# Last attention of a decoder stack: how the queries' maxima reach every partition, and how far the exponentials run behind the scores

## The chip, the cores and the metric

The kernel runs on one core of a Trainium2 chip. The metric is the device time of one execution in microseconds (us). Three runs of the kernel before took 2780.61, 2783.06 and 2793.99 us; the median is 2783.06 us.

## The reference, cut to what matters

A stack of twelve layers (four rounds of self attention, cross attention and a feed-forward part) works on `x` of shape 4 x 256 x 128, with a context of 4 x 1601 x 96. The change touches only the second last layer, a cross attention with 16 heads of 64, which the last layer follows, a linear map whose weights and inputs are whole numbers of eight bits:

```python
def _L3_xattn_ref(x, context, Wq, Wk, Wv, Wo, bo):
    HEADS, DIM_HEAD = 16, 64
    b, n, _ = x.shape                      # 4, 256, 128
    h, d = (HEADS, DIM_HEAD)
    scale = d ** (-0.5)
    q = (x @ Wq).reshape(b, n, h, d).transpose(0, 2, 1, 3)
    k = (context @ Wk).reshape(b, -1, h, d).transpose(0, 2, 1, 3)   # 1601 keys
    v = (context @ Wv).reshape(b, -1, h, d).transpose(0, 2, 1, 3)
    sim = jnp.einsum('bhid,bhjd->bhij', q, k) * scale
    attn = jax.nn.softmax(sim, axis=-1)
    out = jnp.einsum('bhij,bhjd->bhid', attn, v)
    out = out.transpose(0, 2, 1, 3).reshape(b, n, h * d)
    return out @ Wo + bo

x = _layernorm(x + _L3_xattn_ref(x, ctx_768, ...), axis=-1)
x = _layernorm(x + _L3_ffn_ref(x, weight_q, weight_scale, bias), axis=-1)
```

The softmax is over all 1601 keys, and the maximum over the keys is subtracted from each query's scores before the exponential. All of this is in 32-bit floats.

## The kernel before, in words

The kernel is one program of eight stages, one after the other on the same core; the last stage, `l3_xattn`, begins at about 1908 us of the span. A helper, `mm` (L389), issues almost every product of TensorE, so nearly all products carry its line and are told apart by their tiles.

**Units and steps.** The work is cut into 32 units, one batch and one pair of heads each, the two heads standing in the two halves of the 128 partitions. The 1601 keys are 13 chunks of up to 128 keys. A unit takes four steps of up to four chunks; `parts(g)` gives a step's tiles of two chunks each, so steps 0, 1 and 2 of a unit have two tiles and step 3 has one, with the last 65 keys. Scores lie transposed: the keys on the partitions, the 256 queries (two blocks of 128, `NB` = 2) of both heads along the free dimension. One tile `St` holds 2 heads x 2 chunks x 256 queries, 1024 numbers per partition.

**What each part does.** `queries` makes Q of a unit (TensorE; VectorE copies it out of PSUM, L1890). `projections` makes K of the coming step and V of the step whose exponentials are due (ScalarE copies both, L1921). `scores` multiplies Q and K; ScalarE copies each tile from PSUM to `St` in SBUF (L1933). `running` keeps a maximum over the tiles of a unit, element by element, in a place of an old weight tile (VectorE, L1940 and L1943; the trace calls this place w), and at the unit's end joins the two chunks to `mx` (L1947). `maxima` turns that over with products with the identity, so that the queries come onto the partitions, and VectorE reduces over the 128 key partitions (L1959): `mq` has 128 queries on the partitions and 4 columns, one per head and block of queries. `spread` must bring these 512 maxima onto every partition: 8 products of a column of `mq`, broadcast to 64, with the identity put them into a PSUM tile, and ScalarE copies it to `Mb` (L1971). `shifted` subtracts `Mb` from each score tile (VectorE, L1977), `weights` takes the exponential in place (ScalarE, L1984), and `sums` multiplies the exponentials with V and with ones, adding up over a unit in one PSUM tile. At a unit's end the denominators are copied (`rows`, L2016), spread by a product, inverted and multiplied in (VectorE, L2025 and L2028), and after each batch's eighth unit the output projection, the norms and the last layer follow a few instructions at a time (`advance(later)`).

**The order.** TensorE, VectorE and ScalarE run this stage in the order in which it is written (`manual_schedule`), each from its own queue, waiting on semaphores. The loop at the end of `l3_xattn` lays down step g: scores are made for step g, while subtraction and exponential work on step g - LAG and `sums` on the step before that; LAG is 5. There are 12 tiles `St` to hold what lies between. Two PSUM tiles called `one` serve queries, maxima, spread, the sums and the output; three wider ones, `big`, serve projections and scores.

SP issues the DMAs. In this stage it issues only the two small loads at the start and the write of each batch's output (L2112). The weights `Wq`, `Wk` and `Wv` of this stage (pack p4, 3072 columns) lie in the weight slot `w0`, whose widest tenant earlier in the program has 4224 columns.

Of the kernel before, what the change touches and what calls it, by code (L numbers as in the profile page):

```python
# [21 lines left out]
B, T, D = 4, 256, 128  # L22
P = 128
NB = T // P
# [4 lines left out]
NH = 16  # L29
# [15 lines left out]
SW = 32  # L45
# [3 lines left out]
SLOT = {  # L49
    "p0": 0, "down": 0, "p4": 0, "p1": 1, "p3_0": 1, "p5": 1, "p2": 2, "p3_1": 2,  # L50
    "up": 3, "p3_2": 3, "gp": 4, "p3_3": 4,
}

SINGLES = ("l0_xattn", "block1", "l2_xattn", "l2_ffn", "l3_attn")

# [5 lines left out]
class Pack:  # L61


    def __init__(self, width):
        self.a = np.zeros((P, width), np.float32)
        self.at = {}
        self.n = 0
# [236 lines left out]
class Net:  # L304
    def __init__(self, ctx: ExitStack, tc: tile.TileContext, dram, at):
        self.tc, self.nc, self.dram, self.at = tc, tc.nc, dram, at

        def pool(name, bufs, **kw):
            return ctx.enter_context(tc.tile_pool(name=name, bufs=bufs, **kw))

        self.const = pool("const", 1)
        self.wpool = pool("wpool", 1)
        self.act = pool("act", 2)
        self.stage = None
        self.packs = {}
        self.carried = []
        self.n = 0
# [35 lines left out]
    def load(self, name, keep=False, parts=(0,)):  # L353
        src = self.dram[name]
        if keep:
            t = self.tile(name, [P, src.shape[1]], pool=self.const)
        else:
            t = self.tile(f"w{SLOT[name]}", [P, src.shape[1]], pool=self.wpool)
        for lo, hi in zip(parts, parts[1:] + (src.shape[1],)):
            self.nc.sync.dma_start(t[:, lo:hi], src[:, lo:hi])  # L360
        self.packs[name] = t
# [1493 lines left out]
    def l3_xattn(self):  # L1855
# [2 lines left out]

        nc = self.nc
        HD, LAG = 64, 5
        halves = [slice(0, HD), slice(HD, P)]
        wq, wk, wv = self.w("p4", "Wq"), self.w("p4", "Wk", CD), self.w("p4", "Wv", CD)
        units = [(b, hp) for b in range(B) for hp in range(NH // 2)]
        steps = 4 * len(units)
        qs, ks, vs, sts, mx, top, accs, outs = {}, {}, {}, {}, {}, {}, {}, {}
# [5 lines left out]
        kept = self.tile(f"w{SLOT['p3_1']}", [P, 11, T], pool=self.wpool)  # L1873
        one = [kept[:, i].rearrange("p (n d) -> p n d", n=NB) for i in range(8, 11)]
        places = {"h": kept[:, 4:8], "x1": one[0], "x3": one[1], "xn": one[2]}
        self.late = places.get

        def parts(g):

            d = g % 4  # L1880
            for k in range(2 * d, min(2 * d + 2, NCH // 2 + 1)):
                yield k, min(2, NCH - 2 * k), min(P, S2 - 2 * k * P)
# [40 lines left out]
        def scores(g):  # L1923
            u = g // 4
            for k, nc_, kp in parts(g):
                ps = self.big().rearrange("p (h c t) -> p h c t", h=2, c=2)
                for c in range(nc_):
                    o = (2 * k + c - g % 4 * 4) * P
                    for h, r in enumerate(halves):
                        self.mm(ps[:kp, h, c, :], ks[g][r, o : o + kp], qs[u][r, :])  # L1930
                st = self.tile("St", [P, 2, 2, T], bufs=12)
                sts[u, k] = st
                nc.scalar.copy(st[:kp, :, :nc_, :], ps[:kp, :, :nc_, :])  # L1933

        def running(g):
            u = g // 4
            for k, nc_, kp in parts(g):
                if k == 1:
                    mx[u] = kept[:, :4].rearrange("p (h c) t -> p h c t", h=2)
                    nc.vector.tensor_max(mx[u], sts[u, 0], sts[u, 1])  # L1940
                elif k:
                    to = mx[u][:kp, :, :nc_, :]
                    nc.vector.tensor_max(to, to, sts[u, k][:kp, :, :nc_, :])  # L1943
            if g % 4 == 3:
                m = mx.pop(u)
                mx[u] = self.tile("mx", [P, 2, T], bufs=2)
                nc.vector.tensor_max(mx[u], m[:, :, 0, :], m[:, :, 1, :])  # L1947

        def maxima(u):

            ps, m = self.misc(), mx.pop(u)
            for h in range(2):
                for n in range(NB):
                    o = (h * NB + n) * P
                    for d in halves:
                        cols = slice(n * P + d.start, n * P + d.stop)
                        self.mm(ps[d, o : o + P], m[:, h, cols], self.ident)
            mx[u] = self.tile("mq", [P, 2 * NB], bufs=2)
            nc.vector.reduce_max(out=mx[u], in_=ps.rearrange("p (j k) -> p j k", k=P), axis=AX.X)  # L1959

        def spread(u):

            ps, m = self.misc(), mx.pop(u)
            for j in range(2 * NB):
                for d in halves:
                    self.mm(
                        ps[d, j * P : (j + 1) * P],
                        m[:, j : j + 1].broadcast_to([P, HD]), self.ident,
                    )
            top[u] = self.tile("Mb", [P, 2, T], bufs=2)  # L1970
            nc.scalar.copy(top[u].rearrange("p h t -> p (h t)"), ps)  # L1971

        def shifted(g):
            u = g // 4
            for k, nc_, kp in parts(g):
                e = sts[u, k][:kp, :, :nc_, :]
                nc.vector.tensor_sub(  # L1977
                    e, e, top[u][:kp].unsqueeze(2).broadcast_to([kp, 2, nc_, T])
                )

        def weights(g):
            for k, nc_, kp in parts(g):
                e = sts[g // 4, k][:kp, :, :nc_, :]
                nc.scalar.activation(e, e, AF.Exp, scale=HD**-0.5)  # L1984

        def sums(g):
            u = g // 4
            if g % 4 == 0:
                accs[u] = self.misc()
            acc = accs[u]  # L1990
            es = [(k, nc_, sts.pop((u, k))[:kp]) for k, nc_, kp in parts(g)]
            for k, nc_, e in es:
                for c in range(nc_):
                    i = 2 * k + c
                    for h, d in enumerate(halves):
                        if i < NCH - 1:
                            self.mm(
                                acc[d, :T], vs[g][:, i - g % 4 * 4, d], e[:, h, c, :],
                                start=i == 0, stop=False,
                            )  # L2000
            for k, nc_, e in es:
                kp = e.shape[0]
                for c in range(nc_):
                    for h in range(2):
                        d = slice(HD * h + SW * c, HD * h + SW * c + SW)
                        self.mm(
                            acc[d, T:], self.w("c", "ones", kp)[:, :SW], e[:, h, c, :],
                            start=False, stop=False,
                        )
                if kp < P:  # L2010
                    for h, d in enumerate(halves):
                        self.mm(acc[d, :T], vs[g][:kp, 0, d], e[:, h, 0, :], start=False)
            vs.pop(g)
            if g % 4 == 3:
                rows = self.tile("rows", [P, T], bufs=1)
                nc.scalar.copy(rows, acc[:, T:])  # L2016
                later.append(ended(u, rows))
# [32 lines left out]
        with self.tc.manual_schedule(engines=engines):  # L2050
            for g in range(-1, steps + LAG + 2):
                gb = g - LAG
                if g % 4 < 2 and 0 <= g - 1 < steps:
                    running(g - 1)
                if g % 4 == 1 and 4 < g <= steps + 1:
                    spread(g // 4 - 1)
                if 0 <= gb < steps:
                    shifted(gb)
                if 0 <= g + 1 < steps and (g + 1) % 4 == 0:
                    queries((g + 1) // 4)  # L2060
                if g + 1 < steps or gb < steps:
                    projections(g + 1, gb)
                if 0 <= gb < steps:
                    weights(gb)
                self.advance(later)
                if 0 <= gb - 1 < steps:
                    sums(gb - 1)
                if g % 4 == 0 and 4 <= g <= steps:
                    maxima(g // 4 - 1)
                if g % 4 > 1 and 0 <= g - 1 < steps:  # L2070
                    running(g - 1)
                if 0 <= g < steps:
                    scores(g)
            while later:
                self.advance(later)
# [59 lines left out]
```

## Time and profile before

| | |
|---|---|
| median of three runs | 2783.06 us |
| the profiled execution | 2780.11 us |
| its span, first to last instruction | 2778.3 us |
| TensorE busy | 2620.5 us (94%) |
| VectorE busy | 1747.2 us (63%) |
| ScalarE busy | 1526.2 us (55%) |
| mean granted TensorE clock | 0.977 |

The profile gives one execution, with engines named PE (TensorE products), PEld (TensorE weight loads), DVE (VectorE), ACT (ScalarE), POOL (GpSimd) and SP (the engine that issues the DMAs). A group line names the source line, the engine, the operation, output and inputs, the shapes, the count, then after a bar the busy time in us and the mean of one in ns, then the idle time of the engine just before these instructions and what ended it. A timeline line has the start and the length in us, the engine, and in brackets the idle time before. In the row of 40 slices each digit is the busy share of one slice in tenths; a slice is 69.5 us.

### The profile page before, as it was taken

To read this page: it belongs to the slowest core of one execution; us is meant where nothing else is said; L and a number is where in the kernel's file an instruction comes from. 1 tells how busy PE (TensorE), PEld (TensorE's weight loads), DVE (VectorE), ACT (ScalarE), POOL (GpSimd) and SP (SyncE) were. 2 spreads that over 40 slices of the span, in tenths; PEclk is the share of its full clock that TensorE was granted. 3 is DMA by queue.
4 is the path that set the end of the run, shared out by engine and by line. 5 is a ranking of instruction groups with operands and counts; after the bars stand their busy time and mean duration, and the time that the engine had idled before them with its cause. 6 is when DMAs were issued, how large, how long until landed. Compare 5 with 4: busy or idle time off the path is not lost.

```text
span 2778.3 us, 63280 instructions
## 1 busy us (share of the span) xinstructions
PE 2620.5 (94%) x26619; PEld 1707.8 (61%) x26619; DVE 1747.2 (63%) x3802; ACT 1526.2 (55%) x2931; POOL 180.8 (7%) x199
## 2 busy tenths in 40 slices
PE   6999999988879999999997999999999999999997
PEld 4555565555555555555796777776566666666665
DVE  5656666365457666655344666666767777777775
ACT  2555555535533555555553555556666566566563
POOL 2000100120020000000001011101000000000000
PEclk8999999989989999999998999999999999999999
DMA  3000000000020000000002000000000000000000
GB/s 111 2 1 1 2 1 1 3 21 15 26 88 13 6 1 1 1 2 1 1 1 91 15 25 13 12 13 3 2 1 2 3 2 2 3 2 1 3 2 3
DMA packets 12955, 34.57 MB, mean 12 GB/s; under 512 B 3832, under 2 KB 7036, under 8 KB 11264
## 3 DMA queue, kind: packets, MB, share of 16 engines
q1 hardware_dynamic: 12672, 30.53, 3.9%
q8 instruction: 210, 3.44, 0.5%
q14 instruction: 73, 0.60, 0.1%
HBM read 23.67 MB, written 0.52 MB: 9 GB/s over the span
## 4 chain that ended last, share of the span: by engine, by line
PE 88%; DVE 6%; ACT 3%; issue 2%; POOL 1%; DMA 1%; DVEq 0%; POOLq 0%; ACTq 0%
PE one L389 63%; PE big L389 13%; PE acc L389 8%; DVE M L899 1%; PE one L825 1%; PE one L534 1%; PE one L462 1%; DVE St L1977 1%; DVE mpad L687 1%; PE one L1314 1%; ACT E L721 0%; DMA QK<-qk 0%; DVE w L1943 0%; DVE rec L2025 0%; POOL rn L1247 0%
## 5 line engine op out<-in xcount | busy, mean ns | idle before, releaser
L899 DVE TENSOR_REDUCE M<-one 128x1 f32<-128x458 f32 (+3 forms) x1024 | 528.7, 568 | 291.7 <-PE one L389 290.2
L922 ACT ACTIVATE E<-one 128x512 f32<-128x512 f32 (+1 forms) x896 | 457.7, 563 | 422.5 <-PE one L389 422.4
L389 PE MATMUL one<-Q,K 32*128 32x256 f32 (+1 forms) x3328 | 531.9, 402 | 1.5 <-DVE M L899 1.5
L389 PE MATMUL one<-K,Q 32*128 32x458 f32 (+3 forms) x2048 | 458.8, 543 | 1.6 <-DVE M L899 1.6
L389 PEld LDWEIGHTS one<-Q,K 32*128 32x128 f32 (+1 forms) x3328 | 310.7, 180 | 62.4 <-DVE M L899 35.5
L1933 ACT COPY St<-big 128x1024 f32<-128x1024 f32 (+1 forms) x224 | 204.3, 959 | 160.1 <-PE big L389 160.1
L389 PEld LDWEIGHTS one<-K,Q 32*128 32x128 f32 x2048 | 171.1, 186 | 143.3 <-issue 79.7
L1977 DVE TENSOR_TENSOR St<-St,Mb 128x1024 f32<-128x1024 f32 (+1 forms) x224 | 245.3, 1142 | 1.8 <-ACT Mb L1971 1.8
L389 PE MATMUL acc<-E,V 128*32 128x256 f32 (+1 forms) x3328 | 233.2, 387 | 7.1 <-ACT E L922 7.1
L1984 ACT ACTIVATE St<-St 128x1024 f32<-128x1024 f32 (+1 forms) x224 | 215.1, 1014 | 26.0 <-DVE St L1977 25.9
L721 ACT ACTIVATE E<-one 128x384 f32<-128x384 f32 (+1 forms) x352 | 154.3, 525 | 111.9 <-PE one L389 111.7
L389 PE MATMUL big<-Q,K 64*128 64x256 f32 (+1 forms) x1664 | 214.4, 393 | 0.0
L482 POOL TENSOR_TENSOR ln_r<-ln_ve,half 128x2 f32<-128x2 f32 x92 | 70.9, 770 | 2080.0 <-DVE ln_ve L480 2025.7
L389 PE MATMUL one<-St,V 128*64 128x256 f32 (+1 forms) x1664 | 204.1, 382 | 0.4
L1943 DVE TENSOR_TENSOR w<-w,St 128x1024 f32<-128x1024 f32 (+1 forms) x160 | 178.6, 1116 | 35.2 <-ACT St L1933 27.4
L682 DVE TENSOR_REDUCE Ms<-one 128x3 f32<-128x384 f32 x256 | 130.3, 551 | 97.3 <-PE one L389 96.1
L389 PE MATMUL one<-xT,w 128*128 128x256 f32 (+1 forms) x664 | 169.5, 396 | 18.8 <-DVE Q L1117 8.3
L389 PEld LDWEIGHTS big<-Q,K 64*128 64x128 f32 (+1 forms) x1664 | 147.7, 183 | 57.5 <-issue 40.6
L389 PEld LDWEIGHTS acc<-E,V 128*32 128x32 f32 (+1 forms) x3328 | 87.3, 109 | 125.0 <-issue 70.0
L389 PEld LDWEIGHTS one<-St,V 128*64 128x64 f32 (+1 forms) x1664 | 113.5, 137 | 62.7 <-issue 14.6
L389 PE MATMUL one<-QK 32*128 32x256 f32 (+1 forms) x1408 | 110.7, 385 | 24.3 <-DMA QK<-qk 13.7
L389 PEld LDWEIGHTS big<-w,ctx 96*64 96x64 f32 x1664 | 97.1, 137 | 54.0 <-issue 53.9
(308 smaller groups left out, 3733.5 us busy)
## 6 DMA issues: line engine op xcount, KB each, us to landing
w<-in_p SPq DMA_DIRECT2D x4, 1096.0 KB
QK<-qk SPq DMA_DIRECT2D x256, 16.0 KB
rows<-in_ctx_rows SPq DMA_DIRECT2D x4, 630.5 KB
ctx<-in_ctx SPq DMA_DIRECT2D x4, 600.4 KB
w<-in_down SPq DMA_DIRECT2D x1, 2112.0 KB
w<-in_up SPq DMA_DIRECT2D x1, 1632.0 KB
w<-in_gp SPq DMA_DIRECT2D x1, 1632.0 KB
w<-in_p SPq DMA_DIRECT2D x1, 1536.0 KB
```

Of the source, the lines that this page charges most:

```text
L389: self.nc.tensor.matmul(out, lhsT, rhs, start=start, stop=stop)
L462: self.nc.tensor.transpose(ps[:, n * P : (n + 1) * P], x[:, n, :], self.ident)
L482: nc.gpsimd.tensor_tensor(rstd, ve, self.half[:, :NB], ALU.pow)
L534: self.nc.tensor.transpose(ps[:rows, n * P : (n + 1) * P], m4[:, n, :rows], self.ident)
L682: nc.vector.reduce_max(out=m[:, j, :], in_=ps[:, : 3 * P].rearrange("p (s c) -> p s c", c=P), axis=AX.X,)
L721: nc.scalar.activation(es[t, j], ps[:, :w], AF.Exp, scale=scale)
L899: nc.vector.reduce_max(out=ms[i][:, n, j, part : part + 1], in_=ps[:, at : at + hi - lo], axis=AX.X)
L922: nc.scalar.activation(e[:kp, :w], ps[:kp, :w], AF.Exp, scale=scale)
L1933: nc.scalar.copy(st[:kp, :, :nc_, :], ps[:kp, :, :nc_, :])
L1943: nc.vector.tensor_max(to, to, sts[u, k][:kp, :, :nc_, :])
L1977: nc.vector.tensor_sub(e, e, top[u][:kp].unsqueeze(2).broadcast_to([kp, 2, nc_, T]))
L1984: nc.scalar.activation(e, e, AF.Exp, scale=HD**-0.5)
```

## The change

`spread` no longer uses TensorE and ScalarE. The small tile `mq` (128 queries x 4) is written by one DMA to a row in DRAM, in the order query, then head and block, and a second DMA reads that row of 512 numbers back onto all 128 partitions. It lands in one of two places `home`, which are 1024 columns added to the pack p4's tile in the weight slot. `spread` is called right after `maxima`, one step earlier than before. Since the row's fastest index is now head and block, `shifted` reads it with a view that makes the query the inner index, with a step of four elements; for that view the score tiles change their order from head, chunk, query to chunk, head, query, which changes the indices in `scores`, `running`, `weights` and `sums`. LAG becomes 6 and the tiles `St` 14.

```diff
+SPARE = {"p4": 1024}
...
+        self.dram_pool = pool("dram", 2, space=bass.MemoryType.DRAM)
...
-            t = self.tile(f"w{SLOT[name]}", [P, src.shape[1]], pool=self.wpool)
+            wide = src.shape[1] + SPARE.get(name, 0)
+            t = self.tile(f"w{SLOT[name]}", [P, wide], pool=self.wpool)
...
-        HD, LAG = 64, 5
+        HD, LAG = 64, 6
...
+        home = self.packs["p4"][:, 3 * NH * HD :].rearrange("p (i c) -> p i c", i=2)
...
-                st = self.tile("St", [P, 2, 2, T], bufs=12)
+                st = self.tile("St", [P, 2, 2, T], bufs=14)
                 sts[u, k] = st
-                nc.scalar.copy(st[:kp, :, :nc_, :], ps[:kp, :, :nc_, :])
+                nc.scalar.copy(
+                    st[:kp, :nc_, :, :].rearrange("p c h t -> p h c t"), ps[:kp, :, :nc_, :]
+                )
...
-            ps, m = self.misc(), mx.pop(u)
-            for j in range(2 * NB):
-                for d in halves:
-                    self.mm(
-                        ps[d, j * P : (j + 1) * P],
-                        m[:, j : j + 1].broadcast_to([P, HD]), self.ident,
-                    )
-            top[u] = self.tile("Mb", [P, 2, T], bufs=2)
-            nc.scalar.copy(top[u].rearrange("p h t -> p (h t)"), ps)
+            row = self.tile("mrow", [P, 2 * NB], bufs=2, pool=self.dram_pool)
+            nc.sync.dma_start(row, mx.pop(u))
+            top[u] = home[:, u % 2]
+            nc.sync.dma_start(
+                top[u], row.rearrange("t j -> (t j)").unsqueeze(0).broadcast_to([P, 2 * T])
+            )
 
         def shifted(g):
             u = g // 4
+            m = top[u].rearrange("p (t j) -> p j t", j=2 * NB).unsqueeze(1)
             for k, nc_, kp in parts(g):
-                e = sts[u, k][:kp, :, :nc_, :]
-                nc.vector.tensor_sub(
-                    e, e, top[u][:kp].unsqueeze(2).broadcast_to([kp, 2, nc_, T])
-                )
+                e = sts[u, k][:kp, :nc_].rearrange("p c h (n t) -> p c (h n) t", n=NB)
+                nc.vector.tensor_sub(e, e, m[:kp].broadcast_to([kp, nc_, 2 * NB, P]))
...
-                if g % 4 == 1 and 4 < g <= steps + 1:
-                    spread(g // 4 - 1)
...
                 if g % 4 == 0 and 4 <= g <= steps:
                     maxima(g // 4 - 1)
+                    spread(g // 4 - 1)
```

## The prediction

> **What bounds the kernel now.** I read first the page's head and its 40 slices, to see which engine is full where the change works. The last stage fills the slices from about 28 on.
>
> ```profile
> PE 2620.5 (94%) x26619; PEld 1707.8 (61%) x26619; DVE 1747.2 (63%) x3802; ACT 1526.2 (55%) x2931; POOL 180.8 (7%) x199
> ...
> PE   6999999988879999999997999999999999999997
> ...
> DVE  5656666365457666655344666666767777777775
> ACT  2555555535533555555553555556666566566563
> ```
>
> TensorE is full, VectorE at seven tenths. Then the busy times by window over two successive units (one batch and one pair of heads each), with columns stretch, length, PE, PEld, DVE, ACT, POOL, clock, DMA share, GB/s:
>
> ```profile
> 2191.30:2215.88 24.58, 24.58 (x268) 15.44 (x266) 19.82 (x23) 16.86 (x24) 0.00 (x0) 1.00 0.02 7
> 2215.88:2240.46 24.58, 24.58 (x269) 15.43 (x266) 17.93 (x19) 16.85 (x24) 0.00 (x0) 1.00 0.01 2
> ```
>
> A unit takes 24.58 us and TensorE is busy in all of it, at full granted clock: whatever leaves TensorE shortens a unit, until another engine's 17 to 20 us grow past it. Third, the groups of lines between 1990 and 2700 us, for the pieces that the change touches:
>
> ```profile
> L1977 DVE TENSOR_TENSOR St<-St,Mb 128x1024 f32<-128x1024 f32 (+1 forms) x189 | 206.9, 1142 | 0.0
> ...
> L1940 DVE TENSOR_TENSOR w<-St,St 128x1024 f32<-128x1024 f32 x27 | 33.1, 1226 | 64.0 <-ACT St L1933 64.0
> ...
> L389 PE MATMUL one<-c,mq 128*64 128x128 f32 x432 | 29.5, 279 | 0.0
> ...
> L1971 ACT COPY Mb<-one 128x512 f32<-128x512 f32 x27 | 15.8, 586 | 0.0
> ```
>
> Line L1940, the first maximum of a unit, waits 64.0/27 = 2.4 us each time for ScalarE's copies of the scores; that wait is idle time now and returns below. Last, the timeline around `spread`:
>
> ```profile
> 2226.90 0.85 PEld L389 LDWEIGHTS one<-c,mq 128*64 128x64 f32 x16 [0.33 <-issue]
> 2226.91 1.09 PE L389 MATMUL one<-c,mq 128*64 128x128 f32 x16
> 2227.72 0.25 PEld L389 LDWEIGHTS big<-ctx,w 96*64 96x64 f32 x4
> 2227.83 1.03 PE L389 MATMUL big<-ctx,w 96*64 96x512 f32 x4
> ...
> 2228.17 1.23 DVE L1940 TENSOR_TENSOR w<-St,St 128x1024 f32<-128x1024 f32 x1 [2.39 <-ACT St L1933]
> ```
>
> **Removed.** The 8 products of `spread` (16 records) hold TensorE from 2226.90 to 2227.83: 0.93 us per unit, all on the bound, 32 units: 29.8 us. ScalarE's copy L1971, 0.586 us a unit, goes too; ScalarE is busy 16.9 of 24.6 us and waits for TensorE, so this saves nothing by itself.
>
> **Two DMAs per unit, on SP.** SP issues only 4 output writes in this stage, each placed after VectorE work that precedes the next `mq` anyway, so nothing queues behind. No row shows a lone small transfer; the nearest are 16 KB copies of the stage before, issued at 0.62 us (median), whose only visible wait, 13.7 us, is behind three weight loads of over 1 MB each. The Trainium skill (SBUF — State Buffer, The DMA setup-cost knee) gives a fixed 2 us per transfer; two of them, the second moving 128 x 2 KB, make an estimate of 4.6 to 5.8 us. I take 5. Lower end: two issues, 1.2 us. Upper end: 13.7 us.
> What it must beat: after the last product of `maxima`, TensorE has the step's scores (1.93), the next step (projections 1.1, sums 2.8, scores 1.9 = 5.8), the one after (1.0 + 1.1 + 1.9 = 4.1) and queries, projections and `rows` (2.7) before the sums that take a PSUM buffer freed by the Q copy: 14.5 us. The reduction takes 0.8. VectorE must fit, after landing, two subtractions 2.35, two maxima 2.55, two subtractions 2.35 and the Q copy 0.42 = 7.7. So up to about 6 us of transfer is hidden if all durations stay; each us beyond costs about 1 us a unit.
>
> **Lag 6, 14 score tiles.** The sums come one step later, and the space grows with them. At the start, steps without sums are TensorE-bound as well (22.5 us of 25 between 1905 and 1930), so nothing is lost there. At the end TensorE has 5.4 us of older sums and projections to cover reduction, DMAs, first subtraction and exponential (0.8 + 5 + 1.2 + 1.1 = 8.1): a gap of 2.7 us where before stood gaps of 0.8 and 1.5. I take +1 us, between 0 and 4.
>
> **The score tile's new order.** ScalarE's copy now writes runs of 256 in another order. The tail's copy writes such runs already (65x512, 0.58 us) and K's contiguous one of 512 takes 0.59: no cost. The maxima become contiguous; they run at full rate already.
>
> **The subtraction's second operand.** This decides. Before, `Mb` is read in runs of 256 neighbours. Now the DMA delivers (query, head and block), and the subtraction reads it as (head and block, query): step 4 elements, that is 16 bytes, for all 1024 elements. No large VectorE operand in the trace has such a step, so I bound it. The groups by shape of the same two units:
>
> ```profile
> L1977 DVE TENSOR_TENSOR St<-St,Mb 128x1024 f32<-128x1024 f32 x14 | 16.3, 1219 | 0.0
> ...
> L1943 DVE TENSOR_TENSOR w<-w,St 128x1024 f32<-128x1024 f32 x9 | 11.0, 1222 | 0.5
> ...
> L1977 DVE TENSOR_TENSOR St<-St,Mb 65x512 f32<-65x512 f32 x2 | 1.4, 679 | 0.0
> ```
>
> By these rows, 1219 ns for 1024 and 679 for 512 give 1.055 ns an element, and the fully contiguous L1943 has the same rate. Lower end: nothing added; a gain is excluded, since the other operand is the same. Against it stands the skill (SBUF — State Buffer, Specifications): SBUF lines are 16 bytes and full bandwidth needs at least two hits per line. At 16 bytes every read is a new line with one hit. (The page's later note that one may stride "4 fp32" for free reads the other way at just this step.) It gives no price; if two hits per line are full rate, one is half: an estimate of another 1.055 ns an element, 1.08 us per large tile and 0.54 for the tail, a unit 6 x 1.08 + 0.54 = 7.0 us of VectorE. I take the half rate: the mechanism is stated twice, the permissive figure only in passing. Upper end: those 7.0 us.
>
> **The sum.** By the row: TensorE remains the bound with 24.58 - 0.93 = 23.65 us; 2780 - 30 + 1 = 2751 profiled.
> By the rule VectorE needs 17.93 + 7.0 = 24.9 us of work per unit, more than TensorE's 23.65. Nor can it run without a pause: in the step after a unit's end, ScalarE's queue holds two exponentials ahead of the new unit's two score copies. After the second subtraction come an exponential (1.07) and two copies (1.93), about 3.1 us, before L1940 can start; in between VectorE has only the `mq` reduction, 0.7. So the 2.4 us wait, harmless today, joins the loop: 24.9 + 2.4 = 27.3. The transfers have 0.7 less than 3.1 + 1.23 + 1.15 = 4.8 us until VectorE reaches the first subtraction; at 5 us that leaves about 0.2. A unit is 27.5 us, 2.9 more.
> Which units: 3 carry a batch's output work within the loop and take 34.65 us today by TensorE; VectorE there needs 27.5 + about 6.8 of norms and quantization = 34.3, so about +0.5 each. The first 4 overlap the end of the stage before, with TensorE work beyond a unit's: +1.5 each. The other 24: 2.9 x 24 = 70. The first subtraction starts one step later, about 4 us, and now starts the limiting chain. At the end 7 subtractions take 14.3 instead of 7.4, +7, of which I keep 5. Sum: 70 + 6 + 1.5 + 4 + 5 = +86.
> The profiled execution took 2780.11 us (span 2778.3 and 1.8 around it): 2866. The median of the runs, 2783.06, lies 3 us above: **2869 us, +3.1%**. If single terms are off (half rate with a shorter wait, or DMAs of 6 us) this case spans 2830 to 2895.
>
> **Rivals.**
> Full rate at 16 bytes: TensorE stays bound, 2751 to 2757, with the 3 us median offset **2754**; faster. For it: every fp32 operand in the trace runs at one rate, whatever its shape; against it: none has this step.
> Something between: VectorE's 17.93 + 2.4 reach TensorE's 23.65 only with 3.3 added us, 48% more per element, so up to there the gain is nearly whole; at 61% (4.25 us, a large tile in 1.88 us) the unit is 24.58 again. An added half costs a little jitter: **2765**; at that break-even point 2783 plus the later start, about **2790**.
> The transfers late, at full subtraction rate: beyond 6 us the sums wait; at about 6.9 us the 0.93 are gone. At 8 us: (8 - 6 - 0.93) x 32 = +34, **2817**. Against it: two fixed costs of 2 us; for it: 128 pieces of 16 bytes into DRAM and nothing in the trace like it.
> The change not doing what it says: the products do go from TensorE's queue and no projection waits on the DMA into its weight tile's spare columns, so this has no chance worth a number.
>
> **Chances and range.** Half rate 0.60; full rate 0.21; between 0.13, of which 0.06 faster, 0.06 level and 0.01 slower; late transfers 0.06, all slower. A measurement here tells about 0.5%, 14 us, from no change. Faster 0.27, same 0.06, slower 0.67. The range takes in the full-rate case and the likeliest one's own, 2830 to 2895, cut at its upper part: 2750 to 2888. Left out are the ends of both, 1 to 2 in 10.
>
> **What would show it.** Half rate: the group St<-St with the large tile at about 2.3 us; DVE above nine tenths in the last 11 slices, PE there at eight to nine; a unit of 27 to 28 us; L1940 still idle for ScalarE's copies by about 2.4 us; TensorE waiting for the Q copy before the first sums. If the group stands at 1.2 us, the rule as I read it is wrong and the unit should be 23.65. If VectorE's first subtraction of a unit waits for the DMA by several us, the transfers were mis-sized. A subtraction at 1.6 to 1.9 us puts the result near no change.

## The result and the profile after

The kernel after the change takes 2926.69 us (median of 4 runs, 2912.14 to 2929.7), the kernel before beside it 2781.84 us. The ratio is 1.0502, with a 95% interval of 1.0479 to 1.0525: 5.0% slower. The prediction was 2869 us with a range of 2750 to 2888, so the direction was right and the size too small by 58 us, outside the range. The profiled execution of after has a span of 2927.9 us, 149.6 more than before.

First the head of the page after, and the rows of the 40 slices:

```profile
PE 2662.3 (91%) x26107; PEld 1702.6 (58%) x26107; DVE 1920.3 (66%) x3802; ACT 1522.2 (52%) x2899; POOL 177.2 (6%) x199
...
PE   6999999888889999999979999987899889889886
...
DVE  6666666355566666553446666666877887787886
ACT  2555555455435555555535555554555564555653
...
PEclk9999999899999999999989999998999999999998
```

TensorE has 512 product records fewer and yet 42 us more of busy time. In the last stage it stands at eight and nine tenths where it was full, and VectorE went from seven tenths to seven and eight, not to nine: no engine is full any more. The windows of two units, from one `mx` to the next (columns as before: stretch, length, PE, PEld, DVE, ACT, POOL, clock, DMA share, GB/s):

```profile
2280.55:2308.86 28.31, 25.56 (x252) 15.09 (x250) 23.33 (x19) 16.69 (x23) 0.00 (x0) 0.94 0.06 10
2182.55:2210.64 28.09, 25.27 (x254) 15.12 (x250) 23.31 (x18) 16.69 (x23) 0.00 (x0) 0.94 0.06 11
```

A unit that took 24.58 us takes 28.1 to 28.3 here (28.7 in the mean of those without output work). VectorE works 23.3 us of it and stands for 5; the granted clock of TensorE is 0.94 where it was 1.00. The groups by shape, between 1990 and 2840 us:

```profile
L1984 DVE TENSOR_TENSOR St<-St,w 128x1024 f32<-128x1024 f32 x168 | 339.0, 2063 | 25.8 <-DMA w<-mrow 25.7
L393 PE MATMUL one<-St,V 128*64 128x256 f32 x1332 | 196.3, 446 | 73.6 <-DVE Q L1896 73.6
...
L1948 DVE TENSOR_TENSOR w<-St,St 128x1024 f32<-128x1024 f32 x28 | 34.3, 1225 | 65.0 <-ACT St L1939 65.0
L1984 DVE TENSOR_TENSOR St<-St,w 65x512 f32<-65x512 f32 x28 | 31.0, 1109 | 0.0
...
L1951 DVE TENSOR_TENSOR w<-w,St 65x512 f32<-65x512 f32 x28 | 19.3, 688 | 40.2 <-ACT St L1939 39.4
```

Read the third field first: the large subtraction takes 2063 ns where it took 1219, the tail's 1109 where it took 679. Then the last field, over the window's 28 units: the first subtraction waits 25.7/28 = 0.9 us for the second DMA; the first maximum (L1948) waits 65.0/28 = 2.3 us for the score copies, as before. Two more waits count here: TensorE's sums wait 73.6/28 = 2.6 us for the Q copy, which is new, and the tail's maximum waits 39.4/28 = 1.4 us for its scores, where in before it waits 22.2/27 = 0.8 (1990 to 2690 us):

```profile
L1943 DVE TENSOR_TENSOR w<-w,St 65x512 f32<-65x512 f32 x27 | 18.6, 688 | 22.6 <-ACT St L1933 22.2
```

The timeline of one unit of after shows how these last two hang together:

```profile
2297.89 3.98 DVE L1984 TENSOR_TENSOR St<-St,w 128x1024 f32<-128x1024 f32 x2
2298.91 0.60 PE L393 MATMUL one<-rows,c 128*64 128x256 f32 x4
2301.77 0.43 DVE L1896 COPY Q<-one 128x256 f32<-128x256 f32 x1
2302.26 3.33 PE L393 MATMUL one<-St,V 128*64 128x256 f32 x16 [2.75 <-DVE Q L1896]
2305.51 1.32 PE L393 MATMUL one<-St,c 128*32 128x256 f32 x16
2306.77 0.65 PE L393 MATMUL big<-Q,K 64*65 64x256 f32 x4
2307.52 0.58 ACT L1939 COPY St<-big 65x512 f32<-65x512 f32 x1 [4.56 <-PE big L393]
2308.13 0.69 DVE L1951 TENSOR_TENSOR w<-w,St 65x512 f32<-65x512 f32 x1 [1.34 <-ACT St L1939]
```

VectorE lays two slowed subtractions, 3.98 us, ahead of the small Q copy. TensorE finishes at 2299.51 and stands until the copy has freed a PSUM tile. When it starts again, the 16 products with V take 3.33 us, where they take 1.90 elsewhere, and those with ones 1.32 against 1.07. Behind them come the tail's scores, ScalarE's copy and VectorE's maximum, which waits; and only after that maximum does the next unit's turn begin. The granted clock in the gap and behind it:

```profile
2299.51:2302.26 2.75, 0.00 (x1) 0.00 (x1) 2.75 (x4) 2.05 (x4) 0.00 (x0) 1.00 0.00 0
2302.26:2305.51 3.25, 3.25 (x16) 1.56 (x16) 3.17 (x3) 0.70 (x1) 0.00 (x0) 0.56 0.00 0
```

The last three fields are clock, DMA share and GB/s. The stretch without a product is followed by one at 0.56 of full clock. The Trainium skill (TensorE: Matmul & The Clock Gate, Part 1: The HAM clock gate) says that TensorE falls to half its clock after an idle window of about 3.4 us and warns of gaps longer than that; here a gap of 2.75 us was enough. But the length of the gap alone does not decide it. In the same trace the half clock follows a gap of 2.76 us that begins at 2327.82, and does not follow one of 2.87 us that begins at 2355.88:

```profile
2326.55:2329.97 3.42, 1.27 (x20) 0.81 (x16) 3.42 (x2) 2.45 (x4) 0.00 (x0) 1.00 0.00 0
2329.97:2333.38 3.41, 2.80 (x14) 1.66 (x16) 3.38 (x5) 1.06 (x1) 0.00 (x0) 0.50 0.00 0
...
2353.86:2357.28 3.42, 2.02 (x24) 1.16 (x20) 3.42 (x3) 3.04 (x5) 0.00 (x0) 1.00 0.00 0
2357.28:2360.69 3.41, 1.94 (x20) 1.12 (x24) 3.38 (x4) 1.35 (x2) 0.00 (x0) 1.00 0.00 0
2360.69:2364.10 3.41, 3.41 (x44) 1.87 (x44) 3.18 (x4) 0.58 (x1) 0.00 (x0) 1.00 0.00 0
```

These stretches are cut on a grid of 3.41 us, because in each trace here all half clocks of the last stage begin on such a grid, to within 0.01 us; the shares are by the products that the trace records. The first gap leaves one stretch idle to 63% (1.27 us busy of 3.42); the second is spread over two stretches, idle to 41% and 43%. Counted over the last stage of all twelve traces, from 1930 us on: 118 stretches at full clock were idle to 60% or more, and the half clock followed every one; 2807 were idle to less than 45%, and it followed none; of the 46 between, it followed 22. So what counted in these runs is how much of one stretch of the grid is idle.

### The profile page after: what moved, and what is told of

It reads as the page before. It is cut to its first block, busy times and chain, and to the rows that moved or that the text cites. A ratio compares the mean times of both kernels' runs of the same rounds, so it can differ in the third digit from the quotient of the medians.

```text
span 2927.9 us, 62400 instructions
## 1 busy us (share of the span) xinstructions
PE 2662.3 (91%) x26107; PEld 1702.6 (58%) x26107; DVE 1920.3 (66%) x3802; ACT 1522.2 (52%) x2899; POOL 177.2 (6%) x199
## 4 chain that ended last, share of the span: by engine, by line
PE 64%; DVE 21%; DMA 6%; issue 5%; ACT 3%; POOL 1%; SPq 0%; DVEq 0%; ACTq 0%; POOLq 0%
PE one L393 51%; DVE St L1984 10%; PE acc L393 7%; DVE w L1951 4%; DMA w<-mrow 4%; PE big L393 2%; DMA mrow<-mq 2%; DVE M L903 1%; PE one L829 1%; PE one L538 1%; ACT St L1939 1%; PE one L1318 1%; PE one L466 1%; DVE mq L1967 1%; DVE rec L2030 1%
## 5 line engine op out<-in xcount | busy, mean ns | idle before, releaser
L1984 DVE TENSOR_TENSOR St<-St,w 128x1024 f32<-128x1024 f32 (+1 forms) x224 | 422.3, 1925 | 35.8 <-DMA w<-mrow 35.6
L393 PE MATMUL one<-St,V 128*64 128x256 f32 (+1 forms) x1664 | 247.7, 443 | 78.7 <-DVE Q L1896 73.6
L1989 ACT ACTIVATE St<-St 128x1024 f32<-128x1024 f32 (+1 forms) x224 | 223.4, 999 | 172.2 <-DVE St L1984 171.2
L393 PEld LDWEIGHTS one<-St,V 128*64 128x64 f32 (+1 forms) x1664 | 127.9, 157 | 168.7 <-DVE Q L1896 84.5
L1951 DVE TENSOR_TENSOR w<-w,St 128x1024 f32<-128x1024 f32 (+1 forms) x160 | 179.1, 1119 | 57.3 <-ACT St L1939 49.2
L393 PE MATMUL one<-St,c 128*32 128x256 f32 (+1 forms) x1664 | 133.9, 417 | 0.0
L393 PE MATMUL one<-QK 32*128 32x256 f32 (+1 forms) x1408 | 111.3, 385 | 24.6 <-DMA QK<-qk 13.7
```

Source lines behind the costliest of these rows:

```text
L393: self.nc.tensor.matmul(out, lhsT, rhs, start=start, stop=stop)
L1951: nc.vector.tensor_max(to, to, sts[u, k][:kp, :nc_])
L1984: nc.vector.tensor_sub(e, e, m[:kp].broadcast_to([kp, nc_, 2 * NB, P]))
```

## The experiments

All ratios are to the kernel before, run on the same chip beside the variant. "Unit" is the time from one `mx` to the next of a unit without output work.

### The lag alone, on the kernel before

```diff
+SPARE = {"p4": 1024}
...
-        HD, LAG = 64, 5
+        HD, LAG = 64, 6
...
-                st = self.tile("St", [P, 2, 2, T], bufs=12)
+                st = self.tile("St", [P, 2, 2, T], bufs=14)
...
-            top[u] = self.tile("Mb", [P, 2, T], bufs=2)
+            top[u] = home[:, u % 2]
```

> The kernel before with the lag of six steps and the 14 score tiles alone; TensorE still spreads the maxima and the subtraction reads runs. The spread maxima lie in the spare columns of the weight slot, since the two more tiles leave no other room. Theory: the lag costs 0 to 4 us at the end, 2781 to 2787 us. Rival (the later sums, which now take the PSUM tile that the queries use, put a wait in each unit): 0.3 us or more a unit, 2792 us or more.

Measured: 2786.41 us against 2785.18, ratio 1.0007 (0.9993 to 1.0021), unit 24.6 us. The later exponentials and the two more score tiles cost nothing that can be measured.

### The step of four elements alone, without the two transfers

The kernel before, with its products for the spread, LAG 5 and 12 tiles, but with the new order of the score tile; ScalarE writes `Mb` in the order query, then head and block, and the subtraction reads it with the step.

```diff
+            top[u] = self.tile("Mb", [P, 2 * T], bufs=2)
+            nc.scalar.copy(
+                top[u].rearrange("p (t j) -> p j t", j=2 * NB),
+                ps.rearrange("p (j t) -> p j t", j=2 * NB),
+            )
...
+            m = top[u].rearrange("p (t j) -> p j t", j=2 * NB).unsqueeze(1)
```

> The kernel before (TensorE spreads the maxima, lag 5, 12 tiles) with the step alone: the score tiles in chunk-first order, and ScalarE writes Mb query-first so that the subtraction reads it with the step of 16 bytes; no DMA. Theory: large tiles at 2.06 us, VectorE's 24.9 us plus its waits for the maxima and the score copies (up to 3.8) bound the unit at 27 to 29 us, 2870 to 2930 us. Rival (the DMA or the lag is needed for the loss): below 2800 us.

Measured: 2887.36 us, ratio 1.0374 (1.035 to 1.0398), unit 26.4 us, the large subtraction 2073 ns. The step by itself, with no transfer in the stage, makes the kernel before 104 us slower, where the whole change makes it 145 us slower. Its unit is shorter than that of after, since it has no transfer to wait for and its Q copy is seldom late (13.5 us of waiting between 1990 and 2690 us, where after has 67.6).

### The transfer alone: the landed row read in runs

After, with one view changed: the landed row is read as if it lay in runs of 128 queries. This pairs the maxima with other queries, so a query's scores are shifted by another query's maximum.

```diff
-            m = top[u].rearrange("p (t j) -> p j t", j=2 * NB).unsqueeze(1)
+            m = top[u].rearrange("p (j t) -> p j t", j=2 * NB).unsqueeze(1)
```

> The changed kernel with one thing undone: the subtraction reads the landed row of maxima in the order in which it lies, without the step of 16 bytes. The row then stands in the wrong order, so each query is shifted by another query's maximum (the same one for all of its keys); everything else, DMAs, lag and tiles, is as in the changed kernel. Theory (the step's half rate is the whole loss): large tiles back at 1.22 us, TensorE the bound again, a unit of 23.7 us, about 2752 to 2758 us. Rival (the DMAs' 5.6 us or the lag cost the time): subtractions at 1.22 us, but the first one of a unit and TensorE wait for the DMA, 2800 us or more.

Its windows over two units and its group of large subtractions (1990 to 2690 us):

```profile
2218.40:2242.60 24.20, 24.20 (x256) 14.88 (x254) 18.04 (x19) 17.01 (x24) 0.00 (x0) 1.00 0.06 12
2242.60:2266.30 23.70, 23.70 (x250) 14.57 (x248) 18.02 (x18) 16.66 (x24) 0.00 (x0) 1.00 0.04 13
```

```profile
L1984 DVE TENSOR_TENSOR St<-St,w 128x1024 f32<-128x1024 f32 x165 | 194.4, 1220 | 37.7 <-DMA w<-mrow 37.7
```

Measured: 2766.38 us, ratio 0.993 (0.991 to 0.995). TensorE is full again at clock 1.00, and the unit of 23.70 us is the 23.65 that the prediction works out for full rate. The subtraction waits 37.7/27 = 1.4 us per unit for the DMA, longer than in after, and it costs nothing, since VectorE has 18 us of work in 23.7. Everything that after loses therefore follows from the step of 16 bytes, since without it the same transfers and the same lag make a kernel that is faster by 19 us. In after the step costs 160 us (2926.69 against 2766.38), in the kernel before only 104: with a slow subtraction the transfers or the longer lag, harmless without it, cost some 56 us more. No run has the step with a lag of six and without the transfers, so which of the two it is remains open.

### The right order made by the first DMA

After, but the first DMA writes the row in the order head and block, then query, in pieces of 4 bytes, so that the subtraction can read runs.

```diff
+            row = self.tile("mrow", [2 * NB, P], bufs=2, pool=self.dram_pool)
+            nc.sync.dma_start(row.rearrange("j t -> t j"), mx.pop(u))
...
+            m = top[u].rearrange("p (j t) -> p j t", j=2 * NB).unsqueeze(1)
```

> The changed kernel, but the first DMA writes the row in DRAM head-and-block first, in pieces of 4 bytes, so that the landed row can be read in runs. Theory: subtractions at 1.22 us; if the transfer pair takes at most about 6 us, 2752 to 2758 us as in e1; if the 512 small pieces make it longer, about 1 us a unit for each us beyond 6. Rival (rate of the subtraction does not depend on the step): no change against the changed kernel, about 2927 us.

The timeline around one pair of transfers:

```profile
2318.08 0.36 SPq L1973 DMA_DIRECT2D mrow<-mq  x1
2321.59 0.68 DVE L1984 TENSOR_TENSOR St<-St,w 65x512 f32<-65x512 f32 x1
2322.30 0.63 ACT L1989 ACTIVATE St<-St 65x512 f32<-65x512 f32 x1 [0.97 <-DVE St L1984]
2328.37 0.33 SPq L1975 DMA_DIRECT2D w<-mrow  x1
2332.51 2.36 DVE L1984 TENSOR_TENSOR St<-St,w 128x1024 f32<-128x1024 f32 x2 [10.24 <-DMA w<-mrow]
```

Measured: 3071.23 us, ratio 1.1026 (1.1004 to 1.1049). From the first issue to the second, which waits for the row, lie 10.3 us here (median of the 32 units 9.6); with pieces of 16 bytes, in after, the median is 1.5. The subtraction runs at its old 1220 ns and waits 191.4/20 = 9.6 us per unit. This is the prediction's rival of late transfers, brought about on purpose: at some 14 us from issue to landing a unit grows to about 34 us.

### The right order made by ScalarE

After, with one ScalarE copy per unit that puts the row in runs just ahead of the unit's first subtraction.

```diff
-            top[u] = home[:, u % 2]
+            top[u] = home[:, 0]
...
+            if g % 4 == 0:
+                nc.scalar.copy(
+                    home[:, 1].rearrange("p (j t) -> p j t", j=2 * NB),
+                    top[u].rearrange("p (t j) -> p j t", j=2 * NB),
+                )
+            m = home[:, 1].rearrange("p (j t) -> p j t", j=2 * NB).unsqueeze(1)
```

> The changed kernel, with one ScalarE copy per unit that puts the landed 512 maxima in head-and-block-first order (reading them with the step of 16 bytes once), so that the seven subtractions of a unit read runs of neighbours. Theory: the price of the step is paid on 512 elements instead of 6656 and on an engine with room: a copy of 0.6 to 1.1 us on ScalarE, a unit of 23.7 us, 2752 to 2760 us. Rival (DMA or lag): as e1, 2800 us or more; rival (ScalarE's queue held by the copy's wait for the DMA): gaps of TensorE in the second step after the landing, 2770 to 2800 us.

Measured: 2875.57 us, ratio 1.0329 (1.0301 to 1.0357), unit 26 to 27.7 us. The groups between 1990 and 2690 us:

```profile
L1989 DVE TENSOR_TENSOR St<-St,w 128x1024 f32<-128x1024 f32 x144 | 169.6, 1219 | 117.9 <-ACT w L1982 117.9
...
L1982 ACT COPY w<-w 128x512 f32<-128x512 f32 x24 | 27.2, 1133 | 0.0
```

The copy itself is cheap, 1.13 us, on an engine with more than 7 us to spare in a unit, and the subtraction is back at 1219 ns. But the copy stands in ScalarE's queue behind score copies that wait for TensorE, and the first subtraction now waits 117.9/24 = 4.9 us for it. So the Q copy is late again (61.4/24 = 2.6 us of waiting on TensorE), and the half clock comes back, but only in every second unit, although the gap is the same. Two successive units:

```profile
2249.66 3.54 PE L393 MATMUL one<-St,V 128*64 128x256 f32 x16 [2.67 <-DVE Q L1896]
...
2277.86 1.95 PE L393 MATMUL one<-St,V 128*64 128x256 f32 x16 [2.67 <-DVE Q L1896]
```

The units without output work take 27.7 and 27.0 us in turn: two of them are about as long as 16 stretches of the grid of 3.41 us, so that the gap falls on the same two places of it again and again. For the copy, what counts is not what its engine has to spare, but what the queue holds ahead of it.

### The Q copy ahead of the subtractions

After, with two lines of the loop exchanged: `queries` is laid down before `shifted`.

```diff
-                if 0 <= gb < steps:
-                    shifted(gb)
                 if 0 <= g + 1 < steps and (g + 1) % 4 == 0:
                     queries((g + 1) // 4)
+                if 0 <= gb < steps:
+                    shifted(gb)
```

> The changed kernel with the Q copy laid down ahead of the two subtractions of its step on VectorE, so that the sums get their PSUM tile 4 us earlier; the subtractions keep the step of 16 bytes. Theory: TensorE's wait and the halved clock go, VectorE's own loop remains (subtractions 14.3, other work 10.5, the wait of 2.4 for the score copies, 1.0 for the DMA): a unit of 27.0 to 28.2 us, 2870 to 2905 us. Rival (the half rate is only harmful through TensorE's wait): back near 2780 us. Rival (the wait moves elsewhere): no change.

Windows of two units, and the group of the products with V, here between 1990 and 2690 us:

```profile
2258.80:2285.78 26.98, 25.42 (x248) 15.70 (x248) 23.33 (x19) 16.69 (x23) 0.00 (x0) 0.94 0.04 11
2285.78:2312.50 26.72, 24.02 (x248) 14.42 (x248) 23.30 (x18) 16.36 (x23) 0.00 (x0) 1.00 0.05 11
```

```profile
L393 PE MATMUL one<-St,V 128*64 128x256 f32 x1152 | 141.4, 388 | 22.3 <-DVE Q L1896 13.6 <-DVE y L2108 8.1 <-DVE w L1812 0.6
```

Measured: 2878.81 us, ratio 1.0348 (1.0316 to 1.038). VectorE has the same 23.3 us of work; the wait for the Q copy fell to 13.6/24 = 0.6 us, the products are back at 388 ns, and a unit is about 1.5 us shorter. So the late Q copy costs 48 us of the 145. The other 97 are mainly VectorE's longer work and its waits for the score copies and for the transfer. The clock is not always whole here either: in the first of the two units a gap of 2.06 us ahead of the products of `maxima` is followed by 16 products with K in 3.46 us instead of 2.00; in the second a gap of 1.56 us at the same place is not. Of the 16 gaps of 2.0 to 2.2 us in the last stage of this trace only 3 are followed by the half clock.

### More work for TensorE

After, with the products for V done three times more in one step of each unit; the repeats write the same numbers to the same places.

```diff
+                for c in [*range(n)] * 3 if gv % 4 == 1 else ():
+                    o = lo + c * P
+                    for d in halves:
+                        self.mm(
+                            ps[d, 512 + c * P : 512 + (c + 1) * P],
+                            self.ctx_all[:CD, o + d.start : o + d.stop],
+                            wv[:, hp * P : (hp + 1) * P],
+                        )
```

> The changed kernel with more work for TensorE: in the step whose sums wait for the Q copy, the 8 products of V are made three times more (the same products into the same place), some 2.6 us that fill TensorE's idle gap of about 3 us. Theory (after that gap TensorE is granted half its clock, 0.50 in the 2 to 5 us that follow, and the slow sums lie in the loop by the tail's scores and its maximum): without the gap the 16 products of the sums take 1.9 us again instead of 3.3 to 3.7, a unit 28.7 becomes 27.0 to 27.6, and the kernel gets faster by more work, 2880 to 2900 us. Rival (the clock is no part of the loop, VectorE's own work is): no change, 2920 to 2930 us, or slower.

Measured: 2897.58 us, ratio 1.0414 (1.0383 to 1.0446): faster than after by 29 us, with 1536 product records more. The group between 1990 and 2690 us:

```profile
L393 PE MATMUL one<-St,V 128*64 128x256 f32 x1120 | 138.2, 390 | 18.0 <-DVE Q L1896 17.8
```

The products are back at 390 ns, and the gap ahead of them fell from 2.6 us (60.9/23 in the same window of after) to 17.8/23 = 0.8. TensorE comes later to the place where it used to stand, stands there less, and keeps its clock: from 1930 us on the half clock begins 8 times, where it begins 32 times in after. This tells the half clock from a mere wait: had the gap only been waiting, filling it with useless work could not have gained.

### The order mended on VectorE, and the Q copy first

After, with one VectorE copy per unit that brings the row into runs, and `queries` before `shifted`. It computes everything that the kernel before does.

```diff
-            top[u] = home[:, u % 2]
+            top[u] = home[:, 0]
...
+            if g % 4 == 0:
+                nc.vector.tensor_copy(
+                    home[:, 1].rearrange("p (j t) -> p j t", j=2 * NB),
+                    top[u].rearrange("p (t j) -> p j t", j=2 * NB),
+                )
+            m = home[:, 1].rearrange("p (j t) -> p j t", j=2 * NB).unsqueeze(1)
...
```

> The changed kernel with one VectorE copy per unit that puts the landed maxima in head-and-block-first order, behind the DMA's landing and right ahead of the unit's first subtraction, and with the Q copy ahead of the subtractions. Theory: one read of 512 with the step, about 1.1 us a unit on VectorE, which has 5 us of room; subtractions at 1.22 us, TensorE the bound with 23.7 us, as e1: 2755 to 2770 us, faster than the kernel before. Rival (the copy's 1.1 us and the DMA together exceed TensorE's room as ScalarE's copy did in e2): 2790 us or more.

Measured: 2771.61 us against 2783.22, ratio 0.9956 (0.9944 to 0.9968). This run mends two things at once; that the step alone decides is shown by the run with the row read in runs. It reads with the step once, 512 elements in 632 ns, where the score tiles pay 5.5 us a unit for it. And 632 ns is no more than a subtraction of 512 numbers in runs takes (679 ns), so on this copy, which has one input, no price of the step shows; no run has the same copy in runs to compare. The gain is less than the 30 us that leave TensorE: from the first `mx` to the last the kernel takes 789.3 us instead of 810.3, and the end gives back 7.6 of them. The next pair asks about the end.

### The last unit spread by TensorE

In all units but the last the two transfers lie beside other work. The next version spreads the last unit's maxima as the kernel before does, and the version above ran again beside it. (The expectation speaks of 28 units; the stage has 32, and the other 31 keep the transfers.)

```diff
+            if u == len(units) - 1:
+                ps, m = self.misc(), mx.pop(u)
+                for j in range(2 * NB):
+                    for d in halves:
+                        self.mm(
+                            ps[d, j * P : (j + 1) * P],
+                            m[:, j : j + 1].broadcast_to([P, HD]), self.ident,
+                        )
+                top[u] = home[:, 0]
+                nc.scalar.copy(top[u], ps)
+                return
...
```

> This is the version with the VectorE reorder and the Q copy first, but the last of the 28 units spreads its maxima by 16 TensorE products and a ScalarE copy, as the kernel before does; the other 27 units keep the two transfers. Theory (the end pays for the transfers, because no later unit's work covers them, and then for the half clock that follows the wait): the last first subtraction starts about 4 us earlier (its reorder stood 5.10 us behind the transfer), the products behind it run at 1.90 and 1.07 us instead of 3.63 and 1.81, and the end (last mx of the ninth attention to the span's end) falls from 52.5 to 46 to 49 us: ratio to the kernel before 0.993 to 0.9945, against 0.9956 with the transfer for all units. Rival (the end is set by the extra step of lag, not by the transfer): the end stays at 51 us or more and the ratio at 0.9956.

> The version with the VectorE reorder and the Q copy first again, unchanged, beside the version whose last unit is spread by TensorE. Both theories: 0.994 to 0.997 of the kernel before, end 52 to 53 us.

The timeline of the last unit with transfers for all units, and then the same place with the last unit on TensorE:

```profile
2717.01 0.61 DVE L1982 COPY w<-w 128x512 f32<-128x512 f32 x1 [4.93 <-DMA w<-mrow]
...
2721.42 1.12 PE L393 MATMUL one<-rows,c 128*64 128x256 f32 x4 [4.27 <-ACT rows L2026]
2722.33 3.63 PE L393 MATMUL one<-St,V 128*64 128x256 f32 x16
```

```profile
2719.79 1.09 PE L393 MATMUL one<-c,mq 128*64 128x128 f32 x16 [1.63 <-DVE mq L1967]
2720.93 0.59 ACT L1981 COPY w<-one 128x512 f32<-128x512 f32 x1 [0.71 <-PE one L393]
2721.55 4.63 DVE L2001 TENSOR_TENSOR St<-St,w 128x1024 f32<-128x1024 f32 x4 [1.22 <-ACT w L1981]
...
2728.24 1.90 PE L393 MATMUL one<-St,V 128*64 128x256 f32 x16
```

Measured: 2766.06 us with the last unit on TensorE, ratio 0.9933 (0.9921 to 0.9945), and 2771.42 us, ratio 0.9952 (0.9939 to 0.9966), without. The intervals overlap, so the times alone do not settle these 5 us. The traces do: the end, from the last `mx` to the end of the span, is 44.8 us before, 52.1 with transfers for all (52.5 in the profile of the section before), and 47.8 with the last on TensorE. At the end nothing covers a transfer: TensorE stands 4.27 us and then pays again at half clock, 3.63 instead of 1.90 us. The 3 us that are left against before are about what the lag adds there: with the lag alone the end takes 47.4 us. Of the versions that compute what the kernel before does this one has the lowest median.

## Why the prediction came out as it did

**Right: which operand decides.** The step of 16 bytes makes the large subtraction slower, and this alone turns a gain of 0.7% into a loss of 5.0%. TensorE's products do leave the bound for the predicted gain: 23.70 us per unit at full rate, predicted 23.65.

**Mis-sized: the half rate.** The prediction read the Trainium skill's rule (SBUF — State Buffer, Specifications) as exactly half rate, 1.055 ns more per element. Large tile and tail of after give (2063 - 1109)/512 = 1.86 ns against 1.055: 0.81 more, a factor of 1.77. The direction of the rule held for the subtraction, and the page's note that a step of four such elements is free did not. Per unit that is 6 x 0.84 + 0.43 = 5.5 us instead of 7.0. VectorE's work is 23.3 us, not 24.9, and so below TensorE's 23.65: the step that made VectorE the bound by its work alone failed. With the measured subtraction the prediction's own sum, 17.9 + 5.5 + 2.4 + 0.2, gives a unit of 26.0 us; 28.7 were measured, so 2.7 us a unit come mainly from waits that it did not have.

**Mis-sized: the transfers.** The pair takes 5.6 us (in the unit shown, 2.2 from the first issue to the second, 3.4 from there to landing), close to the 5 taken. But the subtraction waits 0.9 us per unit for it, not 0.2.

**The step that failed: what lies in the loop.** "So the 2.4 us wait, harmless today, joins the loop: 24.9 + 2.4 = 27.3." It joined with 2.3 us; but it was not the only one. The prediction itself lists TensorE waiting for the Q copy among the signs, and leaves it out of the sum, as if TensorE's wait lay beside VectorE's. It lies in the loop: two slowed subtractions, Q copy, sums, the tail's scores, ScalarE's copy, the tail's maximum, and from there the next `mx` and the next unit. The chain that ended last, between 2280 and 2310 us of after, runs through just these (start, length, what), after the reduction and the two transfers, 2.13 and 3.37 us:

```profile
2297.97 1.61 DVE St L1984
...
2299.86 2.00 DVE St L1984
2301.87 0.35 DVE Q L1896
...
2302.26 4.58 PE one L393 x32
2306.84 0.60 PE big L393 x4
...
2307.52 0.59 ACT St L1939
...
2308.13 0.70 DVE w L1951
...
2308.86 0.04 DVE mx L1955
```

Of this the 4.58 us contain the half clock: the same products take 1.90 + 1.07 = 2.97 us elsewhere. Added up on VectorE's side, a unit is 23.3 of work, 2.3 for the score copies, 0.9 for the transfer and 1.7 for the maxima L1951, which the late TensorE holds up (46.4 us of waiting over 28 units, by the list of waits): 28.2, against 28.3 in the unit shown. The two errors in the work and in the waits have opposite signs, so that the predicted 27.5 us came as near as they did partly by luck.

**The sum.** From the first `mx` to the last, 31 units, before takes 810.3 us and after 943.9: +133.6, where the terms for the units came to +78. The 21 units without output grew by 4.27 us each, to 28.7, where 2.9 was taken: +29 beyond the prediction. The three pairs with a batch's output work grew from 60.8 to 69.3 us each, +25.6 in all, where 2.9 + 0.5 was taken for a pair: +15. The "+0.5" rested on VectorE's work fitting under TensorE's, but the same waits stand in those units; the 34.65 us, too, are 34.3 by the `mx` of before, and the unit behind, which carries output work as well, takes 26.5. The first four took 18.3 us more, where "+1.5 each" was taken: +12. The end grew by 8.9 instead of 5. By the runs with one part each, the lag alone adds 2.6 there, the step alone 2.9, and the transfers 4.3 (52.1 against 47.8). The first `mx` stands 7.1 us later, but it lies between 1917 and 1936 us in the kernels run here, and at 1917 and 1929 in two executions of the same kernel, so these 7 us are not put down to the change; with them the terms make the 149.6 of the two spans. The 4 us that the prediction took for a later first subtraction cannot be told apart in this sum.

**The range.** Its upper edge was set by single terms that are off one at a time. A loop that several engines share has no room for one late part, and an unpredicted drop of a clock comes with it; 2926.7 lay beyond even the likeliest case's own 2895.

## What to carry to other kernels

A layout that a transfer delivers for nothing is paid for by every instruction that reads it: mend the order once, on the small tile, before many large instructions read it with a step of 16 bytes. When work leaves the full engine, follow the loop from one unit to the next through every queue, and count each wait in it also on the engine that was not the bound, above all a short copy standing behind instructions that get slower. And see that TensorE keeps being fed, since its clock fell behind gaps of two to three us: at the end of a stage, where nothing covers a transfer, the way over TensorE was worth its products.

## What the runs showed of the hardware that was not expected

Gaps on TensorE of 2.06, 2.75 and 4.27 us were followed by products at half clock (3.46 us for 2.00, 3.33 for 1.90, 3.63 for 1.90), but others of 2.06 to 2.87 us were not. What counted was the share of one stretch of a fixed grid of 3.41 us that stood idle: from 60% on the half clock followed always, under 45% never. Because of it, useless products made the kernel 29 us faster.

A VectorE subtraction of 32-bit floats with one of its two operands at a step of 16 bytes costs 1.86 ns an element instead of 1.055. A VectorE copy of 512 elements that it reads at that step takes 632 ns. ScalarE's copy of the same takes 1133 ns, and one that writes 512 at that step (in the run with the step alone) 1132, where its copy into `Mb` in runs takes 586.

Writing 512 numbers to DRAM in 512 pieces of 4 bytes takes 8.7 to 11.2 us from its issue to the issue of the transfer that waits for it, with a median of 9.6; in 128 pieces of 16 bytes, in after, the median is 1.5.
